# A four-layer image network on one core: choice and pooling for layer 2's experts block by block, and an earlier start of layer 3

## The chip, the cores and the metric

The kernel runs on one core of one Trainium2 chip. The metric is the device time of one execution in microseconds (us). The engines that matter are PE (matrix multiply, with its weight load shown as PEld), DVE (vector), ACT (scalar functions), POOL (a third elementwise engine) and SP, which here only issues transfers. Each engine works through its own list of instructions in order, and the engines wait for one another through semaphores. A transfer that an engine issues runs on the DMA engines beside it.

## The reference

The input is x, two images of 64 x 64 places with 128 channels in float32. After normalising it passes four layers, each of which adds to x. For this case two sub-layers matter: the experts of layer 2, which choose 8 of 4096 places for each of 64 experts, and the attention of layer 3 behind them.

```python
t = _to_tokens(x)
t = t + _L2_attn_ref(_ln_t(t), ...)
t = t + _L2_ffn_ref(_ln_t(t), ...)
t = t + _L3_attn_ref(_ln_t(t), ...)
t = t + _L3_ffn_ref(_ln_t(t), ...)

def _L2_ffn_ref(x, gate_w, gate_b, weight1, weight2):
    logits = jnp.einsum('bsd,ed->bse', x, gate_w) + gate_b
    probs = jax.nn.softmax(logits, axis=1)                  # over the 4096 places
    vals, idx = jax.lax.top_k(probs.transpose(0, 2, 1), K)  # K = 8 places per expert
    ...
    pooled = jnp.einsum('bked,bke->bed', gathered, topv)    # weighted sum of the 8 places
    h = jnp.concatenate([pooled.transpose(1, 0, 2), ones], axis=-1)
    h = jax.nn.gelu(jnp.einsum('ebd,edh->ebh', h, weight1), approximate=False)
    h = jnp.concatenate([h, ones], axis=-1)
    out = jnp.einsum('ebh,eho->ebo', h, weight2)
    ...
    weighted = jnp.einsum('beo,bke->bkeo', out, topv).reshape(Bn, K * E, O)
    outputs = outputs.at[jnp.arange(Bn)[:, None], flat_idx].add(weighted)
    return outputs
```

Weights 1 and 2 are 64 matrices each of 128 x 512 and 512 x 128: 32 MB that are read once.

## The kernel before

All of x stays on the chip as a tile of 128 partitions x 64 columns of 128 (column b * 32 + n holds places 128 n to 128 n + 127 of image b). A block is 512 places, four columns; an image has 8 blocks. Layers 0 and 1 take the first half of the time and aren't touched.

**Who decides the order.** The code is Python that records instructions; the framework then puts each engine's instructions in their final order before the run. Earlier in the code means higher priority, but an instruction whose inputs are ready may pass one that isn't. Tiles have a tag and a number of buffers (`bufs`); tiles of one tag take buffers in code order. Tiles live in pools; a pool's place is its tags one after another in order of first use, and a pool that opens when another has closed lies on the same bytes. Its tiles become usable, for the ordering, when the old pool is closed; the wait that remains in the program is only for the old tiles that lie on the same bytes.

**Layer 2's attention** (`layer2_attn`) runs over 16 pairs (image, block), image 0 first, with a list of jobs beside the main loop. Its pools, one above the other on the left, are `l2w` (weights, and before the change the mask `tri`) and `l2a` with the tags xn, xT, q, u, es, selfT, posT and cat, in this order. A large tile on the right, `kept`, which came from layer 1, is cut into keys, values and tables by `take`. PSUM, where PE writes, has the tags misc (2 buffers), sc (2), pos (1) and av (1). For each pair, `join` and `output` add the attention's result to x; `logits(i)` then normalises the block (L172, L1378, L1380), multiplies with the gate weights of 64 experts (`columns`, L1195) and writes 64 rows of logits of 512 places into `pr` (L1385); rows 0 to 63 are image 0, 64 to 127 image 1. The same instruction takes the maximum of the block. The last pair's normalising factor comes from `rsqrt` (L1183 to L1188).

**Layer 2's experts** (`layer2_ffn`) start when all logits are there. Pools: `f2w` (b1, b2, st1, sort, hid, eo, eob), `f2a` (`rest` of 16 KB and xn), and `f2s`, a ring of 12 buffers of 8704 bytes a partition for weights (L1597: 16 loads of 1 MB of weight 1, 16 of weight 2, all issued by SP) and for four zeroed tiles st2. The choice is made on 128 rows x 4096 at once: Exp with its sum (L1620), division (L1622), the 8 largest (L1624), these replaced by 0 (L1626), difference (L1627). The result is transposed (L1635) and pooling multiplies normalised x, computed anew (L172), with it, one image after the other (L1644). The pooled columns go into st1 (L1651), a tile with zeros between, so that windows of 32 columns give one expert's two images each. Then come w1 (L1660), bias and GELU (L1674, L1675), a transpose (L1679, L1681), w2 (L1689), bias (L1697), a re-sorting product (L1700, L1708) and the outputs: chosen weights times expert output for each column (L1719), added to x (L1728), both images in step.

**Layer 3** (`layer3`) opens `l3e`, loads its experts' weights and branches on a value that says whether its scores are bounded; the branch that runs is `l3_bounded`. There `keys(b, g)` (`l3_qkv`) makes statistics, the normalised and transposed block (also the keys), and q for one block; scores (L2076), Exp (L2087) and values (L2035) then run over all pairs of blocks, and later blocks of keys are made beside them.

Of the kernel before, what the change touches and what calls it, by code (L numbers as in the profile page):

```python
# [8 lines left out]
F32 = mybir.dt.float32  # L9
AF = mybir.ActivationFunctionType  # L10
ALU = mybir.AluOpType
# [3 lines left out]
P = 128  # L15
# [24 lines left out]
class Net:  # L40
# [1037 lines left out]
    def layer2(self, kept, done, w3):  # L1078
        nc, tc, ins = self.nc, self.tc, self.ins
        with tc.tile_pool(reuse_waits="tile", name="g2", bufs=1) as gp:  # L1080
# [7 lines left out]

            pr = gp.tile([P, L], F32, tag="pr", name="f2pr")
            mx = gp.tile([P, NC // 4], F32, tag="mx", name="f2mx")  # L1090
            mv = gp.tile([P, B * NC, 2], F32, tag="mv", name="f2mv")
            r = gp.tile([P, B * NC], F32, tag="r", name="f2r")
            gate = gwT, gb, pr, mx, mv, r
            self.layer2_attn(gate, kept, w3)
            done()
            self.layer2_ffn(gate)

    def layer2_attn(self, gate, kept, w3):
# [4 lines left out]
        with ExitStack() as st:  # L1103
# [23 lines left out]
            tri = wp.tile([P, P], F32, tag="tri", name="tri")  # L1127
# [20 lines left out]
            gwT, gb, pr, gmx, gmv, gr = gate  # L1148
# [222 lines left out]
            def logits(i):  # L1371
# [4 lines left out]
                for j in range(4):  # L1376
# [7 lines left out]
                columns(pl[rows], gwT, xT)  # L1384
                nc.vector.tensor_scalar(  # L1385
                    pr[rows, g * 512 : (g + 1) * 512],
                    pl[rows],
                    gb[rows],
                    None,
                    ALU.add,  # L1390
                    ALU.max,
                    accum_out=gmx[rows, g : g + 1],
                )
                yield
# [174 lines left out]
            for _ in logits(last):  # L1569
                pass  # L1570


    def layer2_ffn(self, gate):
# [7 lines left out]
        with ExitStack() as st:  # L1581
            wp = st.enter_context(tc.tile_pool(reuse_waits="tile", name="f2w", bufs=1))
            ap = st.enter_context(tc.tile_pool(reuse_waits="tile", name="f2a", bufs=1))
            ps = st.enter_context(tc.tile_pool(reuse_waits="tile", name="f2p", bufs=3, space=PSUM))
            ws = st.enter_context(tc.tile_pool(reuse_waits="tile", name="f2s", bufs=12))
            _, _, pr, mx, mv, r = gate
# [29 lines left out]

            neg = self.small.tile([P, 1], F32, tag="neg", name="f2neg")
            nc.vector.tensor_reduce(neg, mx, AX.X, ALU.max, negate=True)
            sm = self.small.tile([P, 1], F32, tag="f2sm", name="f2sm")
            nc.scalar.activation(pr, pr, AF.Exp, bias=neg, accum_out=sm)  # L1620
            nc.vector.reciprocal(sm, sm)
            nc.vector.tensor_scalar(pr, pr, sm, None, ALU.mult)  # L1622
            m8 = self.small.tile([P, 8], F32, tag="m8", name="f2m8")
            nc.vector.max(m8, pr)  # L1624
            rest = ap.tile([P, L], F32, tag="rest", name="f2rest")
            nc.vector.match_replace(out=rest, in_to_replace=m8, in_values=pr, imm_value=0.0)  # L1626
            nc.vector.tensor_tensor(pr, pr, rest, ALU.subtract)  # L1627


            prT = ap.tile([P, NC, P], F32, tag="rest", name="f2prT")  # L1630
            for g in range(NC // 4):
                pt = ps.tile([P, 4, P], F32, tag="misc", name=f"f2prT{g}")
                for i in range(4):
                    n = 4 * g + i
                    nc.tensor.transpose(pt[:, i, :], pr[:, n * P : (n + 1) * P], self.ident)  # L1635
                nc.scalar.copy(prT[:, 4 * g : 4 * g + 4, :], pt)
            for b in range(B):
                pp = ps.tile([P, E1], F32, tag="pp", name=f"f2pp{b}", bufs=1)
                for n in range(NC):
                    if n % 4 == 0:  # L1640
                        xn = ap.tile([P, 4, C], F32, tag="xn", name=f"f2xp{b}_{n}", bufs=3)
                    at = b * NC + n
                    self.normalize(xn[:, n % 4, :], self.x[:, at, :], mv, r, at)
                    nc.tensor.matmul(  # L1644
                        pp,
                        lhsT=xn[:, n % 4, :],
                        rhs=prT[:, n, b * E1 : (b + 1) * E1],
                        start=(n == 0),
                        stop=(n == NC - 1),
                    )  # L1650
                nc.vector.tensor_copy(  # L1651
                    st1[:, :, :, b], pp.rearrange("p (j r) -> p j r", j=NT)
                )
# [13 lines left out]
            st2 = []  # L1667
            for c in range(NF):
                s2 = ws.tile([P, NT, NR, WIN], F32, tag="w", name=f"f2st2_{c}")
                nc.gpsimd.memset(s2, 0.0)  # L1670
                st2.append(s2)
# [36 lines left out]
            nc.scalar.copy(eo, pt)  # L1708


            for g in range(NC // 4):
                pts = [
                    ps.tile([P, 4, C], F32, tag="misc", name=f"f2y{b}_{g}") for b in range(B)
                ]
                for i in range(4):
                    n = 4 * g + i
                    for b in range(B):
                        rows = slice(b * E1, (b + 1) * E1)
                        nc.tensor.matmul(  # L1719
                            pts[b][:, i, :],  # L1720
# [5 lines left out]
                for b in range(B):  # L1726
                    xs = self.x[:, b * NC + 4 * g : b * NC + 4 * g + 4, :]
                    nc.vector.tensor_tensor(xs, xs, pts[b], ALU.add)  # L1728
# [28 lines left out]
    def layer3(self, weights):  # L1757
        nc, tc, ins = self.nc, self.tc, self.ins
        G = B * NC
        with ExitStack() as st:  # L1760
# [23 lines left out]
            with tc.If(weights["small"] > 0) as fits:  # L1784
                self.l3_bounded(weights)
# [468 lines left out]
```

## Time and profile before

| | us |
|---|---|
| median of 3 runs (4828.56 to 4833.26) | 4831.08 |
| profiled execution, its own time | 4826.12 |
| its span, first to last instruction | 4824.3 |
| PE busy in it | 4514.4 |
| DVE busy | 2918.7 |
| ACT busy | 2661.0 |
| POOL busy | 945.1 |
| last logits matmul (f2l, L1195) begins | 3599.09 |
| first w1 matmul (f2ph, L1660) begins | 3643.86 |
| bias after w2 (f2eo, L1697) begins | 3704.90 |
| first output matmul (f2y, L1719) begins | 3706.09 |
| first scores of layer 3 (scl, L2076) begin | 3730.34 |

The mean granted PE clock is 0.96 of full speed. The table's lower part gives the points of the stage that the change rewrites, as times from the span's start. Between the last attention work and layer 3's first scores lie some 160 us in which PE isn't full; the rest of the span is untouched by the change, apart from the logits, which are spread over layer 2's attention.

### The profile page before, as it was taken

To read this page: it belongs to the slowest core of one execution; us is meant where nothing else is said; L and a number is where in the kernel's file an instruction comes from. 1 tells how busy PE (TensorE), PEld (TensorE's weight loads), DVE (VectorE), ACT (ScalarE), POOL (GpSimd) and SP (SyncE) were. 2 spreads that over 40 slices of the span, in tenths; PEclk is the share of its full clock that TensorE was granted. 3 is DMA by queue.
4 is the path that set the end of the run, shared out by engine and by line. 5 is a ranking of instruction groups with operands and counts; after the bars stand their busy time and mean duration, and the time that the engine had idled before them with its cause. 6 is when DMAs were issued, how large, how long until landed. Compare 5 with 4: busy or idle time off the path is not lost.

```text
span 4824.3 us, 78221 instructions
## 1 busy us (share of the span) xinstructions
PE 4514.4 (94%) x33260; PEld 1761.8 (37%) x33260; DVE 2918.7 (61%) x4784; ACT 2661.0 (55%) x3091; POOL 945.1 (20%) x848
## 2 busy tenths in 40 slices
PE   6999999999999999978799999999977999999999
PEld 3333333333233333325322223322225444444443
DVE  4676767676766767766746666555553444454447
ACT  4666565655656565555667666676731444433326
POOL 1000000000000000004455454555531000000008
PEclk7999999999999999989899999999987999999999
DMA  1000000000000000000000000000025000000001
GB/s 46 10 1 10 1 10 1 10 1 10 1 1 10 1 12 1 1 6 21 6 1 1 1 1 1 1 1 1 1 93 194 1 1 0 1 0 1 0 1 36
DMA packets 43211, 60.30 MB, mean 12 GB/s; under 512 B 4352, under 2 KB 25056, under 8 KB 41696
## 3 DMA queue, kind: packets, MB, share of 16 engines
q1 hardware_dynamic: 41552, 54.34, 3.6%
q8 instruction: 265, 4.34, 0.4%
q10 hardware_dynamic: 1296, 0.82, 0.1%
q14 instruction: 98, 0.80, 0.1%
HBM read 42.56 MB, written 4.19 MB: 10 GB/s over the span
## 4 chain that ended last, share of the span: by engine, by line
PE 78%; DVE 9%; ACT 6%; POOL 3%; issue 2%; DMA 1%; SPq 0%; DVEq 0%; ACTq 0%; POOLq 0%
PE l0sc L590 17%; PE l0o L549 16%; PE scl L2076 9%; PE oTl L2035 9%; PE l2sc L1448 5%; PE l2pos L1195 5%; PE l2av L1494 3%; DVE l2es L1468 2%; PE f3ex L2185 2%; POOL l2es L1471 2%; PE l0pw L643 1%; ACT l2es L1479 1%; ACT l0es L598 1%; PE l1p L938 1%; ACT l2es L1459 1%
## 5 line engine op out<-in xcount | busy, mean ns | idle before, releaser
L601 DVE TENSOR_TENSOR l0es<-l0es,l0ew 128x1024 f32<-128x1024 f32 x1024 | 1253.4, 1228 | 586.4 <-ACT l0es L598 586.1
L598 ACT ACTIVATE l0es<-l0sc 128x1024 f32<-128x1024 f32 x1024 | 1042.8, 1024 | 676.2 <-PE l0sc L590 671.0
L549 PE MATMUL l0o<-l0es,l0v 64*33 64x512 f32 x8192 | 1068.0, 591 | 19.8 <-ACT l0os L558 12.5
L590 PE MATMUL l0sc<-l0qa,ka 64*64 64x512 f32 x8192 | 1080.6, 596 | 4.7 <-ACT l0es L598 4.7
L1479 ACT ACTIVATE l2es<-l2es 128x1024 f32<-128x1024 f32 (+3 forms) x576 | 559.5, 984 | 265.8 <-POOL l2es L1471 258.7
L1471 POOL TENSOR_TENSOR l2es<-l2es 128x1024 f32<-128x1024 f32 (+3 forms) x352 | 581.2, 1662 | 493.9 <-DVE l2es L1468 442.7
L2043 DVE TENSOR_TENSOR accl<-accl,esl 128x1024 f32<-128x1024 f32 x240 | 302.5, 1261 | 424.6 <-ACT esl L2087 421.2
L1468 DVE TENSOR_SCALAR l2es<-l2sc 128x1024 f32<-128x1024 f32 (+3 forms) x320 | 338.7, 1058 | 314.5 <-PE l2sc L1448 314.3
L2087 ACT ACTIVATE esl<-scl 128x1024 f32<-128x1024 f32 x240 | 245.6, 1023 | 485.2 <-PE scl L2076 460.1
L590 PEld LDWEIGHTS l0sc<-l0qa,ka 64*64 64x64 f32 x8192 | 294.3, 133 | 545.6 <-issue 478.4
L2076 PE MATMUL scl<-l3qT,l3kT 128*128 128x512 f32 x1024 | 487.4, 596 | 0.0
L549 PEld LDWEIGHTS l0o<-l0es,l0v 64*33 64x33 f32 x8192 | 257.2, 108 | 626.8 <-issue 559.2
L1448 PE MATMUL l2sc<-l2q,kept 32*128 32x512 f32 (+3 forms) x2304 | 391.3, 622 | 83.4 <-ACT l2es L1459 58.9
L2035 PE MATMUL oTl<-esl,l3v 128*128 128x512 f32 x960 | 451.1, 592 | 0.0
L724 POOL TENSOR_TENSOR x<-x,l0y 128x256 f32<-128x256 f32 x32 | 23.4, 731 | 2037.1 <-DVE l0y L719 1912.6
L1494 PE MATMUL l2av<-l2es,kept 128*32 128x512 f32 (+3 forms) x2304 | 312.2, 592 | 0.0
L1195 PE MATMUL l2pos<-kept 128*32 128x512 f32 x2416 | 296.8, 599 | 0.1
L2035 PEld LDWEIGHTS oTl<-esl,l3v 128*128 128x128 f32 x960 | 181.7, 190 | 225.6 <-issue 222.0
L2076 PEld LDWEIGHTS scl<-l3qT,l3kT 128*128 128x128 f32 x1024 | 188.2, 191 | 207.5 <-issue 191.3
L1459 ACT ACTIVATE l2es<-l2sc 128x1024 f32<-128x1024 f32 x224 | 226.1, 1010 | 53.2 <-PE l2sc L1448 51.8
L1448 PEld LDWEIGHTS l2sc<-l2q,kept 32*128 32x128 f32 x2304 | 116.1, 187 | 328.3 <-ACT l2es L1459 160.2
L1195 PEld LDWEIGHTS l2pos<-kept 128*32 128x32 f32 x2416 | 78.4, 111 | 175.1 <-issue 174.3
(702 smaller groups left out, 3750.0 us busy)
## 6 DMA issues: line engine op xcount, KB each, us to landing
f2w<-in_L_ffn_weight_dram SPq DMA_DIRECT2D x32, 1024.0 KB, 13.1
l0ew<-l0ew SPq DMA_DIRECT2D x16, 512.0 KB, 5.0
x<-in_x_dram SPq DMA_DIRECT2D x8, 512.0 KB, 8.9
out_dram<-x SPq DMA_DIRECT2D x16, 256.0 KB, 2.3
kept<-in_L_attn_pos_rev_dram SPq DMA_DIRECT2D x1, 1792.0 KB, 6.7
ew<-in_L_ffn_expert_w_dram SPq DMA_DIRECT2D x1, 512.0 KB, 4.0
kept<-in_L_attn_pos_rev_dram SPq DMA_DIRECT2D x1, 256.0 KB
f2b<-in_L_ffn_weight_dram ACTq DMA_DIRECT2D x2, 128.0 KB, 2.7
```

Source lines behind the costliest of these rows:

```text
L549: nc.tensor.matmul(o[64 * h : 64 * h + HD + 1, r, :], lhsT=v1[rows, k, 2 * pair + h, :], rhs=es[rows, h, :], start=(k == 0), stop=(k == NC ...
L590: nc.tensor.matmul(sc[64 * c : 64 * c + 64, h, :], lhsT=ka[rows, k0 : k0 + 64], rhs=qa[rows, k // (NC // 2), qs], start=True, stop=True,)
L598: nc.scalar.activation(es, sc, AF.Exp)
L601: nc.vector.tensor_tensor(es, es, ew[:, :, qs], ALU.mult)
L1195: nc.tensor.matmul(out[part], lhsT=lhsT[:, part], rhs=rhs, start=start, stop=stop)
L1448: nc.tensor.matmul(sc[:, h2, off:], lhsT=kT[hs, k * P : (k + 1) * P], rhs=q[hs, off:], start=True, stop=True,)
L1468: nc.vector.tensor_scalar(es[:, :, lo:], sc[:, :, lo:], root, None, ALU.mult)
L1471: nc.gpsimd.tensor_tensor(part, part, part, ALU.mult)
L1479: nc.scalar.activation(es[:, :, off:], es[:, :, off:], AF.Silu)
L1494: nc.tensor.matmul(avs[i][hs, off:], lhsT=v[:, k, hs], rhs=es[h // 2][:, h % 2, off:], start=(k == 0), stop=last,)
L2035: nc.tensor.matmul(oT, lhsT=vs[b][:, k, :], rhs=es[:, i, :], start=(k == 0), stop=(k == NC - 1),)
L2076: nc.tensor.matmul(sc[:, i, :], lhsT=kTs[b][:, k * P : (k + 1) * P], rhs=qT[:, qb * 512 : (qb + 1) * 512], start=True, stop=True,)
```

## The change

Three things are done. In `logits` the block's maximum is replaced by its 8 largest values, kept in `best`. A new function `choose(b)`, called for image 0 and then image 1 after the last logits and still inside the attention's pools, finds the 8 largest of the 64 kept values of each row, marks all others of `best` with a huge number so that they match nothing, and then goes block by block: Exp (unnormalised, with its sum), replacing the block's chosen values, keeping Exp only where a value was replaced (in place, in `pr`), four transposes, a scaling with the normalising factor of each place while copying, and four pooling matmuls with x itself, not normalised. The mean that normalising would have subtracted, and the softmax's divisor, are applied to the pooled rows at the end; the divisor again to the experts' output (`scale=rs`). It uses the attention's tags: selfT for `e`, posT for `rest`, q for `prT`, misc for the transposes and av for the pooled sum.

In `layer2_ffn` the pool `f2a` is gone, `f2s` has 14 buffers, st1 serves as the first of the four st2 tiles, PSUM tag misc has 4 buffers, and the outputs run image 0 first, then image 1. Between them `begin()` calls `l3_begin`, which opens `l3e` on the right, makes q, keys and the normalised block for block 0 of image 0, and then issues layer 3's loads and memsets. `tri` moves into `kept`.

```diff
-                nc.vector.tensor_scalar(
-                    pr[rows, g * 512 : (g + 1) * 512],
-                    pl[rows],
-                    gb[rows],
-                    None,
-                    ALU.add,
-                    ALU.max,
-                    accum_out=gmx[rows, g : g + 1],
-                )
+                part = pr[rows, g * 512 : (g + 1) * 512]
+                nc.vector.tensor_scalar(part, pl[rows], gb[rows], None, ALU.add)
+                nc.vector.max(best[rows, g, :], part)
                 yield
+
+            def choose(b):
+                rows = slice(b * E1, (b + 1) * E1)
+                all8 = best[rows].rearrange("p g k -> p (g k)")
...
+                nc.vector.max(m8[rows], all8)
+                nc.vector.tensor_scalar(neg[rows], m8[rows, 0:1], -1.0, None, ALU.mult)
+                nc.vector.match_replace(
+                    out=left[rows], in_to_replace=m8[rows], in_values=all8, imm_value=-3e38
+                )
+                nc.vector.tensor_tensor(left[rows], left[rows], all8, ALU.is_equal)
+                nc.vector.scalar_tensor_tensor(
+                    all8, left[rows], 1e30, all8, ALU.mult, ALU.add
+                )
+                pp = ps.tile([P, 512], F32, tag="av", name=f"f2pp{b}", bufs=1)
+                for g in range(NB):
+                    part = pr[rows, g * 512 : (g + 1) * 512]
+                    e = ap.tile([P, 512], F32, tag="selfT", name=f"f2e{b}_{g}", bufs=3)
+                    rest = ap.tile([P, 512], F32, tag="posT", name=f"f2rest{b}_{g}", bufs=3)
+                    nc.scalar.activation(
+                        e[rows], part, AF.Exp, bias=neg[rows], accum_out=ex[rows, g : g + 1]
+                    )
+                    nc.vector.match_replace(
+                        out=rest[rows],
+                        in_to_replace=best[rows, g, :],
+                        in_values=part,
+                        imm_value=-3e38,
+                    )
+                    nc.vector.scalar_tensor_tensor(
+                        part, rest[rows], -1e38, e[rows], ALU.is_le, ALU.mult
+                    )
+                    pt = ps.tile([P, 512], F32, tag="misc", name=f"f2prT{b}_{g}")
...
+                    for i in range(4):
+                        n = 4 * g + i
+                        nc.tensor.transpose(
+                            pt[:, i, :], pr[rows, n * P : (n + 1) * P], self.ident[rows, rows]
+                        )
+                    prT = ap.tile([P, 512], F32, tag="q", name=f"f2prTs{b}_{g}")
...
+                    if g % 2:
+                        for i in range(4):
+                            nc.scalar.activation(
+                                prT[:, i, :],
+                                pt[:, i, :],
+                                AF.Copy,
+                                scale=gr[:, n0 + i : n0 + i + 1],
+                            )
+                    else:
+                        nc.vector.tensor_tensor(
+                            prT,
+                            pt,
+                            gr[:, n0 : n0 + 4].unsqueeze(2).broadcast_to([P, 4, E1]),
+                            ALU.mult,
+                        )
+                    for i in range(4):
+                        nc.tensor.matmul(
+                            pp[rows, :C],
+                            lhsT=prT[:, i, :],
+                            rhs=self.x[:, n0 + i, :],
+                            start=(g == 0 and i == 0),
+                            stop=(g == NB - 1 and i == 3),
+                        )
+                mean = self.small.tile([P, 1], F32, tag="f2mean", name=f"f2mean{b}", bufs=1)
+                nc.vector.tensor_reduce(rs[rows], ex[rows], AX.X, ALU.add)
+                nc.vector.reciprocal(rs[rows], rs[rows])
+                nc.vector.tensor_reduce(mean[rows], pp[rows, :C], AX.X, ALU.add)
+                nc.vector.tensor_scalar(mean[rows], mean[rows], 1.0 / C, None, ALU.mult)
                 nc.vector.tensor_scalar(
+                    pooled[rows], pp[rows, :C], mean[rows], rs[rows], ALU.subtract, ALU.mult
                 )
...
             for _ in logits(last):
                 pass
+            for b in range(B):
+                choose(b)
...
-            ap = st.enter_context(tc.tile_pool(reuse_waits="tile", name="f2a", bufs=1))
-            ps = st.enter_context(tc.tile_pool(reuse_waits="tile", name="f2p", bufs=3, space=PSUM))
-            ws = st.enter_context(tc.tile_pool(reuse_waits="tile", name="f2s", bufs=12))
+            ps = st.enter_context(tc.tile_pool(reuse_waits="tile", name="f2p", bufs=4, space=PSUM))
+            loads = st.enter_context(ExitStack())
+            ws = loads.enter_context(tc.tile_pool(reuse_waits="tile", name="f2s", bufs=14))
...
+            pt = ps.tile([P, C], F32, tag="misc", name="f2poolT")
+            nc.tensor.transpose(pt, pooled, self.ident)
+            nc.vector.tensor_copy(
+                st1[:, :, :, :B], pt.rearrange("p (b j r) -> p j r b", b=B, j=NT)
+            )
...
-            nc.scalar.copy(eo, pt)
+            nc.scalar.activation(eo, pt, AF.Copy, scale=rs)
+
+            loads.close()
+            for b in range(B):
+                rows = slice(b * E1, (b + 1) * E1)
+                for g in range(NC // 4):
+                    pt = ps.tile([P, 4, C], F32, tag="misc", name=f"f2y{b}_{g}")
...
                     xs = self.x[:, b * NC + 4 * g : b * NC + 4 * g + 4, :]
+                    nc.vector.tensor_tensor(xs, xs, pt, ALU.add)
+                if b == 0:
+                    begin()
...
+    def l3_begin(self, st, w):
...
+        wp = st.enter_context(tc.tile_pool(reuse_waits="tile", name="l3e", bufs=1, side="right"))
...
+        with (
+            tc.tile_pool(reuse_waits="tile", name="l3b", bufs=1) as ap,
+            tc.tile_pool(reuse_waits="tile", name="l3bps", bufs=2, space=PSUM) as ps,
+        ):
+            for _ in self.l3_qkv(ap, ps, w, 0, 0, w["qT"], w["kT"], w["vx"], "l3b"):
+                pass
+        w["ew"] = self.load(
+            wp, "ew", [P, E2, C], ins["L3_ffn_expert_w"].rearrange("e d c -> d e c")
+        )
...
-            for g in range(NB):
+            for g in range(1, NB):
                 jobs["keys", 0, g] = keys(0, g)
```

## The prediction, made before the changed kernel was run

> **What bounds the kernel now.** I read four views in this order. First the page's strips of 40 slices (120.6 us each): they show where the tensor engine (PE) isn't full.
>
> ```profile
> PE   6999999999999999978799999999977999999999
> DMA  1000000000000000000000000000025000000001
> GB/s 46 10 1 10 1 10 1 10 1 10 1 1 10 1 12 1 1 6 21 6 1 1 1 1 1 1 1 1 1 93 194 1 1 0 1 0 1 0 1 36
> ```
>
> PE is at 9 tenths nearly everywhere. The one hole in the second half is slices 29 and 30 of 0 to 39 (3498 to 3739 us), the only ones with real DMA traffic: the change's stage. Second, the chain of work that ended last (start, length, engine, tile, line), cut to that stage:
>
> ```profile
> 3599.09 1.95 PE f2l L1195 x4
> 3602.31 3.81 ACT f2pr L1620 x2
> 3606.35 2.36 DVE f2pr L1622
> 3608.73 4.44 DVE f2m L1624
> 3613.26 4.50 DVE f2rest L1626 x2
> 3617.79 4.44 DVE f2pr L1627
> 3622.36 5.49 PE f2prT L1635 x32
> 3627.85 5.84 PE f2pp L1644 x53
> 3635.36 8.08 PE f2pp L1644 x64
> 3643.86 10.03 PE f2ph L1660 x89
> 3653.89 27.58 DMA f2w<-in_L_ffn_weight_dram x2
> ...
> 3688.67 14.33 DMA f2w<-in_L_ffn_weight_dram
> ...
> 3730.34 4.43 PE scl L2076 x8
> ```
>
> So: choice and pooling until 3643.8, expert matmuls that soon wait for weights until 3704.9, outputs and the start of layer 3 until 3730.3. Third, the stretches of that stage (busy us of PE, weight load, DVE, ACT, POOL, then PE clock, DMA share, GB/s):
>
> ```profile
> 3602.00:3622.40 20.40, 0.04 (x1) 0.07 (x2) 18.95 (x19) 3.80 (x2) 0.00 (x0) 0.50 1.04 387
> 3622.40:3643.80 21.40, 20.62 (x160) 20.30 (x160) 13.93 (x54) 5.60 (x9) 0.00 (x0) 0.92 0.02 7
> 3661.60:3704.90 43.30, 29.13 (x520) 21.21 (x516) 1.58 (x5) 0.63 (x1) 0.00 (x0) 0.58 0.96 356
> ```
>
> The weights flow while DVE chooses, stop while PE pools (DMA share 0.02), and then PE waits for them. Fourth, what SP's queue, which issues all 32 loads (L1597), waited for:
>
> ```profile
> SPq L1597 <- PE f2ph L1660: 45.7, 9, 32.8
> SPq L1597 <- PE l2po L1414: 30.4, 1, 30.4
> SPq L1597 <- PE l2av L1494: 4.9, 1, 4.9
> ```
>
> The first load goes out at 3556.59, when the last attention product (L1494) is done; the second waits 30.4 us until the last read of `kept` (L1414) and goes at 3587.40; 12 loads in 12 buffers are in by about 3623, and the next waits 32.8 us for a consumed buffer. From 3647 on the stream is unbroken: the last w1 matmuls start at 3659.92, the last w2 matmuls at 3703.05, so 43.13 us for 16 loads of 1 MB, 2.696 us each. The stage is thus bound first by choice and pooling (42 us from 3601.8), then by the 20 loads left.
>
> **What the Trainium skill says.** "DMA: Bandwidth & Descriptors", Anatomy of one DMA: "DMA engines do not wait on semaphores"; any wait is taken by the issuing sequencer before it dispatches. Hence one load that must wait holds all loads behind it on SP. The trace agrees: the 30.4 us above held loads that nothing else held. "TensorE: Matmul & The Clock Gate", What's actually happening: half clock until about 3.4 us of sustained work. The trace agrees: granted clock 0.50 while PE idles, 0.92 in the pooling stretch. "ScalarE: Activation LUTs", What ACT_TABLE_LOAD costs: 1283 ns; the trace has 1283.
>
> **Part by part.**
>
> (1) Max of each block. Each of 16 blocks' L1385 was 0.756 + 0.080 (accumulator read). Now it is a plain add from PSUM (copies of 512 take 0.685) and a MAX8 of 512: L1624's 4.427 us for 4096 scales to 0.55, with a fixed part 0.62. That is +0.47 us each, 7.5 us of DVE. In 3400 to 3557 DVE is busy 60%, which hides most; but between 2500 and 3557 PE waited 17.3 us for L1468's scaled scores, so some shows: +1 (0 to 3). Image 0's choice begins with five small operations of 0.2, which fall in such gaps too.
>
> (2) Where the first load goes. This decides. Bytes per partition above the base that attention and expert pools share: without `tri`, l2w takes 4992; then l2a has xn 4096, xT 6144, so `q` lies at 15,232 to 19,328. f2w takes 14,848. Before, f2a's 22,528 came next, so the first f2s buffer lay at 37,376, among `es`: the early load at 3556.59 shows that. Now f2a is gone; the first buffer is 14,848 to 23,552, on top of `q`, and `q` is where choose() puts its transposed choices, until the last pooling matmul of image 1. All loads become issuable when the attention's pools close and then go in code order, as before, so the other 31 queue on SP behind the first, whichever buffers they have (most lie in `kept`, free since 3587), and the 128 f2ph matmuls wait for it. All 32 MB now start after pooling, which hides none of them; two more buffers can't mend that. The four bias loads (f2b) on ACT's queue, 0.6 each, also move behind choose()'s ACT work; they are needed after the w1 matmuls, 45 us later: nothing.
>
> (3) The tail before the last logits. Image 0's DVE work (8 x (0.09 value load + 0.6 replace + 0.61 multiply) = 10.4 us) can fill DVE's gaps there, but only from 3571.93, when the last `posT` is taken, since `rest` uses that tag's buffers in order. Gaps between 3572 and 3602 are 30.0 - 19.26 = 10.7 us, the largest 4.6 at 3582.8. It fits in sum, but the work isn't divisible: between the small dependent steps of L1184 to L1188 (0.17 each) an operation of 0.6 may slip in, and ACT gets Exp between two Sqrt (table loads 1.28). I take +5 for the tail (bounds 1, nearly all in gaps, and 8).
>
> (4) Choice and pooling after the last logits' matmul. `misc` banks also go in code order, so no transpose of choose() precedes that matmul; 16 blocks remain for PE. Four transposes: 0.34 (the four of L1378 take 0.66 with the last one's latency); four matmuls of two passes: f2y's passes (1.53 us for 16) give 0.096 each, so 0.77. 16 x 1.1 = 17.6; half clock for the first 3.4 us of work adds 3.4; `av` is one bank, so image 1's pooling waits until image 0 is reduced from it, five small DVE steps, some 1.2; latency 0.3: 22.5. DVE beside it: image 1's 10.4, eight scalings of 256 at 0.42, two tails, prelude 1.2: about 18, hidden. ACT: eight Exp at 0.78, eight times four copies at 0.2: 13, hidden. If evacuations don't keep up with two `misc` banks it's 29; if image 0 runs wholly before, 18. The one-shot stage (42 us) goes.
>
> (5) Weights after that. First bytes 1.9 us after issue (3587.40 to 3589.3), 32 x 2.696 = 86.3, landing 1.5 (3701.5 to 3703.05), last matmuls 1.85: 91.6. Pooled values' transpose, w1 matmuls, GELU, three memsets and buffer releases (14 in flight) lie under the stream.
> L1697 started at 3704.90. Now: 3601.1 + 5 + 22.5 + 91.6 = 3720.2, so +15.3.
>
> (6) Outputs and layer 3. Before, L1697 to the first scores is 3704.9 to 3730.34 = 25.4: both images' outputs in step (DVE 16 x 0.685, PE waiting for banks), then 9.7 for the first block's stats, normalise, transpose, qT. Now image 0's outputs (8 x 0.77), the first block's q and k, and image 1's outputs share the engines: DVE 2.2 + 16 x 0.67 + 4.3 = 17.2, scores at about 16.5: -8.9. But blocks 1 to 7 of layer 3 start only behind image 1's adds on DVE; before, block 1's keys were ready (3730.9) with block 0's. Block 1 needs about 7.5 us (stats 1.7, table load and Sqrt, 1.3, 1.1, transpose, copy 0.6), scores want it 6.9 after the first: about 2.4 lost. Net -6.5 (-9.5 to -3). On POOL the first block's bias add (L1882, 1.30) now stands before the three memsets, on SP the five expert loads of layer 3 (`ew`, `eb`) still come after the weights: both are needed at the experts, near 4700, so they cost nothing.
>
> Sum: +1 + 15.3 - 6.5 = +9.8 us. The profiled execution's span is 4824.3 and its time 4826.1; with +9.8 it would be 4835.9. The median of the runs, 4831.08, is 5.0 above it; I add the difference to the median: 4841.
>
> **Rivals.** (A) Loads start early after all, because the first buffer isn't on `q` or SP doesn't keep code order; not slower. 14 loads stream from about 3592, the last 18 follow when pooling (3628.6) frees buffers: 3628.6 + 2 + 18 x 2.696 + 1.5 + 1.9 = 3682.5, or -22; with (6) and (1) about -27: 4804. For: the old stream did run from 3587. Against: the bytes above. It decides wherever the first load issues before 3605. (B) Choice is short: tail 1, stage 18 and full layer-3 gain: 9.8 - 4 - 4.5 - 3 = -1.7: 4829. For: 10.7 us of gaps. Against: in-order banks. (C) Evacuations set the pace and PE falls to half clock: f2po's matmul groups, busy under three quarters, ran at 0.58. Tail 8, stage 29 and more: +25: 4856.
>
> **How the numbers follow.** 0.2% is 9.7 us, about what a measurement can tell from no change. Forecast 0.81 (own 8-in-10 range 4832 to 4853): slower 0.47, within 0.33, faster 0.01. A 0.10, faster. B 0.05, within. C 0.04, slower. Together faster 0.11, same 0.38, slower 0.51. Range 4826 to 4858: bounds of the terms, B and most of C; A is left out.
>
> **What would show it.** Right: no weight bytes before the last f2pp matmul, then some 86 us without a break and PE waiting for DMA in both expert matmuls; f2eo near 3720; the first scl 16 to 19 us after it, with a PE gap before the third pair of scores. Wrong: a load issued before 3605 (A), f2pp ending before 3620 (B) or after 3636 (C), or L1468's waits grown by several us, which would put the loss into attention.

## The result: slower by 0.85%, and the profile after

The changed kernel took 4870.45 us (4868.30 to 4873.82, 4 runs) against 4829.82 (4826.80 to 4833.26, 4 runs): a ratio of 1.0085, 95% interval 1.0067 to 1.0102. The forecast was 4841, with a range of 4826 to 4858. The profiled execution is at the upper end, 4873.82, with a span of 4871.9; its difference to the span before is 47.6. Cut at the same events in both traces (first and last L1195 / L1198 for l2pos, last f2l, last f2pp, f2eo, first scl), with what the prediction's terms give for the same stretches:

| stretch | before | after | difference | forecast |
|---|---|---|---|---|
| until layer 2's attention starts (code unchanged) | 2338.1 | 2343.5 | +5.4 | 0 |
| attention, to the last l2pos | 1233.2 | 1239.1 | +5.9 | +1.0 |
| tail, to the last logits f2l | 28.7 | 34.8 | +6.1 | +5.0 |
| choice and pooling, to the last f2pp | 43.2 | 29.6 | -13.6 | -19.6 |
| weights, to f2eo | 61.7 | 93.8 | +32.1 | +29.9 |
| outputs, to the first scl | 25.4 | 34.1 | +8.7 | -8.9 |
| the rest | 1094.0 | 1097.0 | +3.0 | +2.4 |
| sum | | | +47.6 | +9.8 |

The first row is scatter: the first l2pos lay between 2337.7 and 2343.0 in the twelve other profiles of this study. It accounts for most of the gap between 47.6 and the medians' 40.6.

The strips of 40 slices (121.8 us each) show the hole of the stage again, now with all weight traffic in slice 30:

```profile
PE   6999999999999999977899999999977999999999
DMA  1000000000000000000000000000007000000001
GB/s 46 10 1 10 1 10 1 10 1 10 1 1 10 1 12 1 1 6 20 6 1 1 1 1 1 1 1 1 1 16 269 1 0 0 1 0 1 1 1 35
```

The chain of waits, cut to the stage (start, length, engine, tile, line):

```profile
3616.53 1.95 PE f2l L1198 x4
3618.51 0.77 DVE f2pr L1389
3619.32 0.69 PE f2prT L1434 x4
3620.01 3.60 PE f2pp L1456 x16
...
3632.45 1.96 PE f2pp L1456 x16
...
3645.39 1.91 PE f2pp L1456 x16
3647.35 6.10 DMA f2w<-in_L_ffn_weight_dram
...
3724.33 14.43 DMA f2w<-in_L_ffn_weight_dram
3738.80 1.98 PE f2po L1734 x32
3741.15 0.81 PE f2sort L1745 x2
3742.40 19.31 PE f2y L1762 x92
```

Before, transfers already ran while DVE chose. Now pooling ends, and only then the first load goes out (3647.35). And where the chain before went from the expert outputs to the scores in 25.4 us, it now spends 19.31 in f2y alone, with more f2y after it. The three stretches (columns as before: span, busy PE, weight load, DVE, ACT, POOL, then clock, DMA share, GB/s):

```profile
3618.40:3647.00 28.60, 26.15 (x193) 22.43 (x192) 17.71 (x45) 14.73 (x49) 0.00 (x0) 0.83 0.00 1
3647.00:3740.80 93.80, 59.58 (x648) 24.13 (x646) 2.73 (x9) 1.91 (x2) 6.13 (x4) 0.58 0.99 362
3740.80:3774.90 34.10, 32.42 (x137) 28.69 (x137) 14.35 (x38) 3.13 (x5) 1.69 (x4) 0.50 0.06 16
```

No byte flows beside pooling (DMA share 0.00), then the stream is unbroken (0.99), and the outputs run with PE busy and its clock at 0.50. SP's waits name the first load's last obstacle (time in total, times, longest):

```profile
SPq L1675 <- DVE f2prTs L1449: 1319.4, 1, 1319.4
SPq L1675 <- PE f2pp L1456: 2.4, 1, 2.4
```

### The profile page after: what moved, and what is told of

The parts are those of the page before. It is cut to its first block, busy times and chain, and to the rows that moved or that the text cites. A ratio compares the mean times of both kernels' runs of the same rounds, so it can differ in the third digit from the quotient of the medians.

```text
span 4871.9 us, 78359 instructions
## 1 busy us (share of the span) xinstructions
PE 4554.7 (93%) x33293; PEld 1782.7 (37%) x33293; DVE 2927.2 (60%) x4790; ACT 2682.1 (55%) x3152; POOL 945.2 (19%) x847
## 4 chain that ended last, share of the span: by engine, by line
PE 77%; DVE 10%; ACT 6%; POOL 3%; issue 2%; DMA 2%; SPq 0%; ACTq 0%; DVEq 0%; POOLq 0%
PE l0sc L590 17%; PE l0o L549 16%; PE scl L2131 9%; PE oTl L2090 9%; PE l2sc L1524 5%; PE l2pos L1198 4%; PE l2av L1570 3%; PE f3ex L2238 2%; DVE l2es L1544 2%; POOL l2es L1547 2%; PE l0pw L643 1%; ACT l2es L1555 1%; DMA f2w<-in_L_ffn_weight_dram 1%; ACT l0es L598 1%; PE l1p L938 1%
## 5 line engine op out<-in xcount | busy, mean ns | idle before, releaser
L1198 PE MATMUL l2pos<-kept 128*32 128x512 f32 x2416 | 295.6, 597 | 0.1
L1198 PEld LDWEIGHTS l2pos<-kept 128*32 128x32 f32 x2416 | 78.2, 111 | 173.8 <-issue 172.9
```

Source lines behind the costliest of these rows:

```text
L1198: nc.tensor.matmul(out[part], lhsT=lhsT[:, part], rhs=rhs, start=start, stop=stop)
```

## The experiments

Times are medians, ratios are against the kernel before in the same session. "Steps" are the sixteen additions of l2po (L1422 before, L1498 after), which cut the attention into stretches.

### Where the loads stood: e1_gap, e5_gap_bias, e6_own

e1_gap:

```diff
+            wp.tile([P, 1120], F32, tag="gap", name="f2gap")
             w1 = [weights(1, e) for e in range(NR)]
```

> The changed kernel with 4,480 unused bytes per partition in the pool f2w, so that the 14 weight buffers begin above the tile q (prT of choose) and no longer on it; nothing else. Theory (the first buffer on q holds every load back): the first load issues near 3605, when the last attention projection has freed kept, eight loads stream during choice, the ninth and tenth (on selfT and posT) wait until the last e and rest are read, near 3643, the other 24 follow without a break: L1742 at about 3714 instead of 3740.8, the whole 20 to 28 us faster than the changed kernel (about 4846). Rival (all loads wait for the attention's pools to close, whatever lies where): first issue stays near 3647 and the time within 3 us of 4870.

4861.73 (4849.60 to 4863.70), ratio 1.0063 (1.0046 to 1.0080). The first load went at 3595.8, so `q` had held all of them. But only four got through; SP's waits of e1_gap:

```profile
SPq L1675 <- DMA f2b<-in_L_ffn_weight_dram: 42.4, 2, 42.0
SPq L1675 <- PE f2ph L1706: 2.9, 4, 1.9
```

SP stood 42.0 us, before the fifth load, for a transfer of f2b, a bias. ACT issues those behind the choice's copies, at 3640.26. In the trace's records the fifth load and the first bias load name the same semaphore (104) for their completion. f2eo came at 3724.9 and not at 3714. Neither theory had this second lock. (The text of the next run says that five loads got through and the sixth stood; the trace has four and the fifth.)

e5_gap_bias adds:

```diff
-                nc.scalar.dma_start(out=b1[b::2], in_=ins["L2_ffn_weight1"][:, C, :])
-                nc.scalar.dma_start(out=b2[b::2], in_=ins["L2_ffn_weight2"][:, FF, :])
+                nc.sync.dma_start(out=b1[b::2], in_=ins["L2_ffn_weight1"][:, C, :])
+                nc.sync.dma_start(out=b2[b::2], in_=ins["L2_ffn_weight2"][:, FF, :])
```

> e1_gap with the four bias loads f2b issued on SP behind the sixteen loads of w1 instead of on ACT; nothing else. In e1_gap five loads went out from 3595.8 and the sixth stood until the bias loads, which ACT issues behind the choice's work at 3640, had landed. Theory (loads on both queues share a few completion counters in turn, so a late bias load on ACT stops SP too): now eight loads go out early, the ninth waits for the last e and rest near 3642, L1742 at about 3712 instead of 3724.9, the whole about 4845. Rival (the sixth load waited for something else, the tile u or es): stall at the same place, L1742 near 3725, time near 4858.

4840.16 (4827.24 to 4843.46), ratio 1.0021 (1.0014 to 1.0028): 30 us off the change by two edits that remove no work. SP's waits of e5_gap_bias:

```profile
SPq L1675 <- DVE f2pr L1427: 22.8, 1, 22.8
SPq L1675 <- PE f2ph L1706: 5.8, 4, 4.7
```

The bias is gone from the list, as the theory of shared counters says. Eight loads go early; the one long stop left is for the last read of e and rest (L1427), as expected, though it ended at 3635.0 and not near 3642. f2eo: 3706.5.

e6_own keeps the bias edit and takes choose() off every weight buffer:

```diff
+            gap = loads.enter_context(tc.tile_pool(reuse_waits="tile", name="f2g", bufs=1))
+            gap.tile([P, 5680], F32, tag="gap", name="f2gap")
-            ws = loads.enter_context(tc.tile_pool(reuse_waits="tile", name="f2s", bufs=14))
+            ws = loads.enter_context(tc.tile_pool(reuse_waits="tile", name="f2s", bufs=13))
...
-                    e = ap.tile([P, 512], F32, tag="selfT", name=f"f2e{b}_{g}", bufs=3)
-                    rest = ap.tile([P, 512], F32, tag="posT", name=f"f2rest{b}_{g}", bufs=3)
+                    both = ap.tile([P, 2, 512], F32, tag="u", name=f"f2er{b}_{g}", bufs=3)
+                    e, rest = both[:, 0, :], both[:, 1, :]
```

> e5_gap_bias with 13 weight buffers that begin above q and u, and with e and rest in the tile u, so that nothing of choose() lies under a weight buffer; the rest is the change. Theory (only choose's tiles and the bias loads kept the stream back): 13 loads go out from about 3600 without a stop, 19 are left when pooling ends near 3647, L1742 at about 3703, the whole about 4833, 37 us faster than the change. Rival (choice and stream disturb each other, or something else holds SP): a stop before the 13th load, L1742 after 3712, no faster than e5_gap_bias.

4846.67 (4844.06 to 4849.79), ratio 1.0039 (1.0025 to 1.0053). The stream did as expected: 13 loads before pooling ended. The time didn't follow, for two reasons. From the last f2pp to f2eo it took 61.6 us, hardly less than with eight early loads (62.2 in e5_gap_bias): the 13 buffers were full, and the 14th load waited until 3651.2, behind the first w1 matmul at 3650.1. And the attention grew by 12.7 more than in e1_gap (last l2pos 1251.9 after the first, against 1239.2). ACT's timeline in e6_own, inside the attention, shows why:

```profile
3520.26 1.28 ACT L1418 ACT_TABLE_LOAD   x1
3521.55 0.72 ACT L1418 ACTIVATE f2er<-f2pr,f2neg 64x512 f32<-64x512 f32 x1
...
3523.18 0.71 ACT L1418 ACTIVATE f2er<-f2pr,f2neg 64x512 f32<-64x512 f32 x1
3523.79 0.19 ACT L1418 ACTIVATION_READ_ACCUMULATOR f2er<-f2pr,f2neg 64x1 f32 x1
3524.00 1.28 ACT L1555 ACT_TABLE_LOAD   x1
```

`e` used `selfT`, and in the change the buffers of that tag, which go in code order, had kept image 0's first Exp back until 3568.1. Here it starts at 3506.2: two Exp slip in between the attention's own activations and cost two table loads, five times. A resource taken away let work in where it hurt.

### The outputs: e2_in_step, e7_block

e2_in_step puts the passes of both images in step again, as in the kernel before. With that, layer 3's first block (`begin()`) comes behind both images and no longer between them:

```diff
-            for b in range(B):
-                for g in range(NC // 4):
-                    for i in range(4):
+            for g in range(NC // 4):
+                for i in range(4):
+                    for b in range(B):
...
-                if b == 0:
-                    begin()
+            begin()
```

> The changed kernel with the output matmuls f2y of both images in step again (rows 0 to 63 and 64 to 127 in turn, as in the kernel before), layer 3's first block after them; nothing else. Theory (turns between the row halves let one pass's weights load beside the other's matmul): a pass of f2y costs 0.095 us instead of 0.22, all 128 take 12 to 14 us, L1742 to the first scl goes from 34.1 to about 25, the whole 7 to 10 us faster (about 4862). Rival (PE comes out of the load stage at half clock and stays there; order of passes is nothing): passes keep 0.2 us, granted clock stays 0.50, the time within 3 us of 4870.

4853.81 (4852.91 to 4855.81), ratio 1.0051 (1.0035 to 1.0068): 16.6 off the change by order, more than expected. f2eo to the first scl: 18.5. The group f2y in the change and in e2_in_step (duration in ns as min/median/max, first and last start):

```profile
L1762 PE MATMUL f2y<-f2eob,f2pr x128: 417/417/579, 3742.4 to 3773.6; 64*128 64x128 f32 x128
```

```profile
L1764 PE MATMUL f2y<-f2eob,f2pr x128: 271/272/579, 3742.1 to 3754.8; 64*128 64x128 f32 x128
```

The same 128 passes start within 12.7 us instead of 31.2. The move of `begin()` can't be the reason, since the six matmuls of it that stood among them kept PE busy for under 4 us. Two things are in it, the overlap of the row halves and the clock. Two stretches of e2_in_step (columns as above):

```profile
3742.10:3746.00 3.90, 3.90 (x36) 3.90 (x38) 1.83 (x6) 1.21 (x1) 0.00 (x0) 0.50 0.37 110
3750.00:3754.80 4.80, 4.28 (x48) 3.40 (x47) 4.58 (x14) 0.00 (x0) 0.00 (x0) 1.00 0.00 0
```

At 0.50 a pass in step takes 3.90 / 36 = 0.108 us. In the change, one image after the other and at 0.50 too, it was 19.31 / 92 = 0.210 in the chain above. So there is an overlap of the row halves, which the rival denied. It is that of whole passes: in step the records mostly show two of them, one on each half, starting 5 to 7 ns apart, and the next two 213 ns later; in the change single passes follow every 213 ns. The theory's weight load beside a matmul isn't what differs: in the change, too, 115 of 128 weight loads start 5 ns after the start of the matmul before them.

What the clock is worth can't be read from the second stretch, 4.80 / 48 = 0.100, for there the passes wait for DVE (busy 4.58). The pooling passes show it. In the change they run alone: 16 took 3.60 us at 0.50 and 1.91 at 1.00 (chain above). In e8_all, below, those of the two images run in pairs, on halves of the columns; from its chain of waits, the first at 0.50 nearly throughout, the second at 1.00:

```profile
3614.22 3.41 PE f2pp L1451 x32
3622.36 1.99 PE f2pp L1451 x32
```

So pairs are worth a factor of about two, and so is the clock. By these prices, as an estimate, the 128 passes of f2y would take 15.3 us one at a time at 1.00 (128 x 1.91 / 16), and 13.6 in pairs at 0.50 (64 x 0.213) if they waited for nothing; neither was run as such. The change had neither pairs nor full clock; e2_in_step has the pairs from the start and full clock after some 5 us. What the clock alone does to passes in step, the kernel before (1.00) and e3_best, below (0.50), show with the same code: 0.109 and 0.136 us a pass, waits included.

```profile
3706.00:3720.00 14.00, 12.16 (x128) 10.63 (x128) 9.61 (x16) 0.04 (x1) 0.39 (x1) 1.00 0.00 1
```

```profile
3724.00:3730.00 6.00, 6.00 (x44) 5.86 (x44) 2.62 (x5) 0.00 (x0) 0.00 (x0) 0.50 0.01 3
```

e7_block asks what brings the clock up:

```diff
-            eo = wp.tile([P, C], F32, tag="eob", name="f2eob")
+            eo = wp.tile([P, B, C], F32, tag="eob", name="f2eob")
...
+                    nc.tensor.matmul(
+                        pt[:, i, :, :],
+                        lhsT=pr[:, n * P : (n + 1) * P],
+                        rhs=eo,
+                        start=True,
+                        stop=True,
+                    )
```

> The changed kernel with the outputs of both images in one matmul: pr of all 128 rows against a 128x256 operand that holds each image's expert rows in its own half and zeros elsewhere, 32 matmuls of 256 columns instead of 64 of 128; layer 3's first block after them. Theory A (passes on 64 rows in turn don't bring the granted clock up, passes on all rows do): clock at 1.00 within 5 us of the first pass, outputs in 10 to 13 us, L1742 to the first scl 17 to 20: about 4854, as e2_in_step. Theory B (the clock stays low after the load stage whatever the passes are): clock 0.50 throughout, outputs 18 to 21 us, L1742 to the first scl 25 to 28, about 4861.

4858.92 (4854.66 to 4859.77), ratio 1.0062 (1.0045 to 1.0078). In the profiled execution, the fastest of the four, the clock did what A says; stretches of e7_block from f2eo on (columns as above):

```profile
3735.00:3741.00 6.00, 4.70 (x15) 3.48 (x12) 1.28 (x4) 2.01 (x3) 0.70 (x3) 0.50 0.01 3
3741.00:3744.00 3.00, 3.00 (x13) 2.52 (x12) 2.35 (x7) 0.00 (x0) 0.00 (x0) 0.80 0.02 5
3744.00:3750.00 6.00, 6.00 (x30) 5.28 (x29) 5.57 (x17) 0.20 (x1) 0.00 (x0) 1.00 0.00 0
```

It rose some 5 us after the first pass at 3737.3. But the outputs took 16.1 us: 64 passes of 256 columns, half of the operand zeros, are dearer than 128 in step, and the time lies between A and B. In the five kernels with image after image (the change, e1_gap, e4_both, e5_gap_bias, e6_own) the clock stayed at 0.50 for all of some 31 us; of the seven in step, three came to the outputs at 1.00, three were there some 5 us after the first pass, and e3_best stayed at 0.50 for some 17 us. Each is one profiled execution. What the clock counts stays open.

### The best of each block, and both images at once: e3_best, e4_both

e3_best puts two lines of the change into the kernel before:

```diff
-                nc.vector.tensor_scalar(
-                    pr[rows, g * 512 : (g + 1) * 512],
-                    pl[rows],
-                    gb[rows],
-                    None,
-                    ALU.add,
-                    ALU.max,
-                    accum_out=gmx[rows, g : g + 1],
-                )
+                part = pr[rows, g * 512 : (g + 1) * 512]
+                nc.vector.tensor_scalar(part, pl[rows], gb[rows], None, ALU.add)
+                nc.vector.max(gmx[rows, g, :], part)
```

> The kernel before with only the change's best of each block: a plain add and a MAX8 of 512 in place of the add with accumulated maximum, 16 times (tri stays where it was, the choice is the old one). Theory 1 (the MAX8s on DVE hold up the attention; they are the 5.9 us by which the attention grew): 4834 to 4837 against 4830. Theory 2 (they lie in DVE's gaps, the growth came from where the granted clock fell in that execution): within 2 us of 4830.

4839.86 (4835.09 to 4842.96, 16 runs), ratio 1.0021 (1.0014 to 1.0029): 12 us, more than either theory. Its profile, of an execution at the upper end, has 4.5 in the attention; the largest later piece, 5.5, is from f2eo to the scores, where its in-step passes took 18.4 us, most of it at clock 0.50, against 13.2 at 1.00 in the kernel before. Both have three PSUM buffers there, the change has four. In the attention the loss comes in steps: 0.26 until step 5, then 2.9 in one. There PE's clock differs; two stretches (columns as above) of the kernel before, and of e1_gap, whose attention starts at nearly the same time:

```profile
2807.00:2809.00 2.00, 2.00 (x15) 0.92 (x17) 1.59 (x3) 0.00 (x0) 0.00 (x0) 1.00 0.00 0
2809.00:2811.00 2.00, 2.00 (x24) 0.52 (x16) 1.43 (x2) 0.69 (x1) 0.43 (x1) 1.00 0.00 0
```

```profile
2807.00:2809.00 2.00, 2.00 (x9) 1.59 (x10) 1.11 (x2) 0.00 (x0) 0.00 (x0) 0.50 0.00 0
2809.00:2811.00 2.00, 2.00 (x8) 0.20 (x8) 1.27 (x3) 0.00 (x0) 0.00 (x0) 0.50 0.00 0
```

After a stall that both have, the clock is back at 1.00 within 4 us in the one and after 10 in the other. All nine kernels with MAX8s on image 0's blocks show the long form; of the four without, one does too (e11_gate). So the long form goes with the MAX8s, put in here with the plain add, but it isn't theirs alone; why the clock comes back so late stays open.

e4_both calls choose() once, on all 128 rows:

```diff
-            for b in range(B):
-                choose(b)
+            choose()
...
-                    nc.scalar.activation(
-                        e[rows], part, AF.Exp, bias=neg[rows], accum_out=ex[rows, g : g + 1]
-                    )
+                    nc.scalar.activation(e, part, AF.Exp, bias=neg, accum_out=ex[:, g : g + 1])
...
                     for i in range(4):
-                        nc.tensor.matmul(
...
+                        for b in range(B):
+                            rows = slice(b * E1, (b + 1) * E1)
+                            nc.tensor.matmul(
```

> The changed kernel with the choice of both images at once, block by block on all 128 rows (half as many replaces, multiplies and exponentials), all of it after the last logits; loads and outputs as in the change. Theory (image 0's choice in the tail costs what it takes, since it pushes between the small steps of the last logits): the tail is again that of the kernel before (6 us shorter), choice and pooling after the last logits about 25 instead of 28.8: 7 to 11 us faster than the changed kernel. Rival (the work of image 0 really is in gaps, and only the order that puts it there keeps the stage short): the stage grows to 32 to 36, the whole 0 to 3 us slower.

4858.20 (4855.87 to 4860.06), ratio 1.0061 (1.0045 to 1.0078): 12 off the change. Tail 28.8, as in the kernel before: there the theory holds, and image 0's work had cost what it took. Choice and pooling, last f2l to last f2pp, 22.1 against 29.6. That is no proof for the halved DVE work, since the edit also lets the pooling passes of both images alternate, so that they run in pairs (32 in 1.98 us at clock 1.00): in this stretch PE is busy 14.9 instead of 27.2 us, DVE 15.6 instead of 17.7. What each is worth wasn't separated.

### Together: e8_all, e9_mend, e10_late, e11_gate

e8_all is e4_both, e6_own's places, e2_in_step's order and, in logits:

```diff
-                nc.vector.max(best[rows, g, :], part)
+                if b == B - 1:
+                    nc.vector.max(best[:, g, :], pr[:, g * 512 : (g + 1) * 512])
```

> e4_both, e6_own and e2_in_step together, and the best of each block taken for both images at once when the second image's logits come (8 MAX8 of 128 rows instead of 16 of 64). Theory (the change's loss is the sum of those pieces): attention 2 to 5 us longer than in the kernel before, first load before 3600, pooling done near 3631 beside an unbroken stream, L1742 at 3687 to 3694, first scl 18.5 later, 4808 to 4820: faster than the kernel before by 8 to 20 us. Rival (pooling and the stream share something, or the buffers come free too late): L1742 no earlier than 3703, 4825 or more.

4804.25 (4802.87 to 4804.84), ratio 0.9947 (0.9930 to 0.9963): faster than both kernels and 4 below the range expected. Its three stretches (pooling, weights, outputs; columns as above):

```profile
3605.10:3627.40 22.30, 15.15 (x162) 12.49 (x160) 15.64 (x38) 13.01 (x49) 0.62 (x2) 0.73 1.04 382
3627.40:3689.20 61.80, 44.66 (x651) 25.61 (x648) 2.73 (x10) 1.75 (x2) 5.62 (x3) 0.70 0.90 329
3689.20:3706.40 17.20, 13.64 (x137) 10.39 (x137) 14.83 (x51) 3.22 (x6) 2.10 (x4) 1.00 0.12 33
```

The stream now fills the pooling stretch (1.04), f2eo is 15.7 earlier than in the kernel before, and the outputs run at clock 1.00. Choice and stream now lie beside each other.

e9_mend is the change with e1_gap's, e5_gap_bias's and e2_in_step's edits only.

> The change with three small edits and nothing else: the gap in front of the weight buffers, the bias loads on SP behind those of w1 (both as in e5_gap_bias), the outputs of both images in step (as in e2_in_step). Theory (both losses are independent, so they add): e5_gap_bias 4840 less the 15 to 16 that e2_in_step gained on the change, 4824 to 4828, no slower than the kernel before. Rival (with the earlier end of the load stage PE comes to the outputs at another clock, as in e3_best, where the same order of passes ran at 0.50 and took 18 us): 4830 to 4836.

4823.03 (4819.45 to 4826.30), ratio 0.9987 (0.9979 to 0.9996). The two losses add: three edits that remove no work take 47 us off the change.

e10_late and e11_gate ask what the MAX8s left in e8_all cost. e10_late moves them to the start of choose(); e11_gate puts a copy ahead of them that reads the last logits but one:

```diff
+                g = order[-2][1]
+                nc.vector.tensor_copy(
+                    best.rearrange("p g k -> p (g k)"), pr[:, g * 512 : g * 512 + 64]
+                )
+                for g in range(NB):
+                    nc.vector.max(best[:, g, :], pr[:, g * 512 : (g + 1) * 512])
```

> e8_all with the best of each block taken only at the start of the choice (8 MAX8 of 128 rows, none in the attention). Theory (a MAX8 in the attention costs more than its 0.69 us since it shifts PE's waits and with them the granted clock): the attention is again that of the kernel before, 3.9 us shorter than in e8_all; seven of the MAX8s find gaps between the small steps of the last logits, the eighth is on the path, 0.7: about 4801. Rival (they stand in the way of the last logits as image 0's choice did in the change): tail 3 to 5 us longer, 4803 to 4807, no gain.

> e10_late with the eight MAX8s held back by one small copy that reads the last logits but one, so that none can stand in the attention (in e10_late five of eight stood there all the same, as soon as their logits were there, and the attention's steps were those of e8_all). Theory (the MAX8s, not the plain add or anything else of the change, lengthen the attention in e8_all): every step of the attention is within 0.2 us of the kernel before, 3.9 us shorter than in e8_all; seven MAX8s of 0.69 stand between the last two blocks of logits, where DVE has some 3 us free, so 1 to 3 of it is given back: 4801 to 4803 against 4804.25. Rival (something else moved the attention): the steps stay those of e8_all and the time rises to 4805 to 4807.

e10_late: 4803.00 (4800.06 to 4805.79), ratio 0.9944 (0.9927 to 0.9960), which tests nothing: the framework put five of the eight back into the attention as soon as their logits were there, and its steps equal e8_all's within 0.1. e11_gate: 4806.90 (4803.05 to 4808.05), ratio 0.9952 (0.9936 to 0.9969). The time is the rival's, the steps are those of neither text. The attention is 1.5 longer than in the kernel before (4.0 in e8_all), of which 1.26 arose before any logits; what e8_all loses from step 12 on, where its MAX8s stand, is gone, so they were its cause. But the tail is 3.0 longer. Saved in one place, given back in the next.

## Why the prediction was wrong, step by step

**(2) and (5), loads: right in mechanism and nearly in size.** +32.1 against +29.9. `q` held the first load and code order the rest (e1_gap). The side remark that the bias loads on ACT cost "nothing" was wrong as a mechanism, though hidden here by `q`: with `q` free they cost 21.1 between the last f2pp and f2eo (83.3 in e1_gap, 62.2 in e5_gap_bias). Rival A, loads early, didn't occur.

**(6), the step that failed: the price of the output passes, taken over from (4), "f2y's passes (1.53 us for 16) give 0.096 each".** With it PE's part, twice "image 0's outputs (8 x 0.77)" or 12.3 us, lay hidden under DVE's 17.2, and the forecast had scores 16.5 after f2eo. It was 34.1, 17.6 of the 32.4 us by which the terms missed beside the scatter. The 0.096 was read where two images' passes ran mostly in pairs, on rows 0 to 63 and 64 to 127, at clock 1.00. The change puts 64 passes of one image after another on the same rows, and the clock, for which the term had nothing, stayed at 0.50: 0.210 each, so PE set the pace (busy 32.42 of 34.10). The Trainium skill, "TensorE: Matmul & The Clock Gate", Part 3, The mechanism, says that a weight load overlaps with running matmuls "only when row_grp differs". The trace doesn't agree: the 115 loads above begin beside a matmul on the same rows. What no longer overlapped were the passes. e2_in_step undoes it, pairs and clock at once; as estimated there, either alone would have brought most of it. With the passes in step, f2eo to scores is 18.5 and the gain of layer 3's early start is real, even behind both images: -7.0 there, +1.1 in the rest, against -6.5 forecast. The step overlooked was that a loop's order, and the clock that came with it, were part of the price.

**(4), choice and pooling: a size.** 29.6 against 23.6 from the last f2l's start. The same 0.096 was used for the pooling passes, which run alone: at 1.00 16 of them took 1.96 (0.1225 each), 128 x 0.0265 = 3.4 more. The clock stayed at 0.50 for 9.7 us, not 3.4 (the first 32 passes took 3.60 and 3.67). That loses 4.9, estimated as half of the 9.7; the forecast had put in 3.4, by the same count twice what 3.4 us at 0.50 lose, so 1.5 more. The last 1.1 wasn't traced.

**(1), MAX8 in the attention: a size.** +5.9 against +1, outside its bounds of 0 to 3. e3_best shows 4.5 for the MAX8s and plain adds alone; another 1.5 is there at step 15 (counted from step 1, e3_best +4.1, the change +5.6) and wasn't traced. A block cost DVE 0.61 more, not 0.47, but the sum of DVE times and its busy share said little: what counted was how PE's waits shifted and what the clock made of it.

**(3), the tail: right.** +6.1 against +5 (1 to 8), and e4_both gives it back whole. **The rest** +3.0 against +2.4.

Rival B, a short choice, didn't occur either. Rival C was near in size, a stage of 29 against 28.8 from the end of the last f2l, and had PE at half clock, as it was for 10 us; but in the main PE, busy 26.15 of 28.60, set the pace and not the evacuations. The outputs, where most of the missing time lay, were priced with paired passes at full clock in every case.

## What to carry to other kernels

A duration read from a trace belongs to its neighbours: before it prices the same instruction elsewhere, ask what ran beside it and at which clock, above all for matmuls on half the rows or columns. Where transfers are issued in order, list everything that lies on the first buffer and every transfer that shares completion counters with it, on other queues too. Work put into gaps should be checked against the alternative of doing it once on all rows: here that was worth 12 us, together with the paired passes that it brought.

## What the runs showed of the hardware that wasn't expected

Passes one at a time on 64 rows kept PE busy for 31 us without the clock leaving 0.50, in five of five kernels; passes on 128 rows raised it within some 5 us in one. The Trainium skill, "TensorE: Matmul & The Clock Gate", What's actually happening, has full clock after about 3.4 us of sustained work; these stretches don't agree, so a busy PE isn't enough. Two passes on separate halves of the rows or columns start within 5 to 7 ns and run together: 32 took 1.99 us where 16 alone took 1.91. After one stall in the attention nine kernels had 10.2 us at 0.50 where the kernel before has 3.4, and lost 2.9; in six of them the work had shifted by no more than 0.3 us until then. A transfer queued on SP waited 42.0 us for one that ACT had to issue, into other bytes; both name one semaphore for their completion, and moving it to SP ended that wait.
